# Planning the order of a whole kernel by repeated list scheduling, with new weights for its operations

## The chip, the cores and the metric

The kernel runs on one core of one Trainium2 chip. The metric is the time of one launch on the device, in microseconds (us). Five engines work side by side, each through its own instructions in the order in which they stand in the program: TensorE (PE, with its weight loads shown as PEld), VectorE (DVE), ScalarE (ACT), GpSimd (POOL) and SyncE (SP), which here only issues transfers. Engines wait for each other by semaphores.

## What is computed

Two layers over an input of shape (8, 192, 64, 64), that is 8 images of 192 channels and 64 by 64 places, all in float32. Cut to what matters:

```python
# layer 0: attention in windows of 8x8, only the 16 largest scores of each row, then an MLP
shortcut = layer_norm(tokens)
q, k, v  = windows(shortcut) @ qkv_w.T                 # 6 heads of 32
attn     = l2n(q) @ l2n(k).T * temperature
attn     = where(attn >= 16th largest of its row, attn, -100)
attn     = softmax(attn + relative_position_bias)
x2       = shortcut + (attn @ v) @ proj_w.T
x2       = x2 + gelu(layer_norm(x2) @ fc1_w.T) @ fc2_w.T
# layer 1: a small MLP on the 2-D Fourier coefficients of each channel, then an MLP
f  = fft2(layer_norm(x2))                              # over 64 x 64, each channel
x3 = x2 + real(ifft2(mlp_of(real(f), imag(f))))        # 2 -> 16 -> 2, gelu
out = x3 + gelu(layer_norm(x3) @ mlp1_w.T) @ mlp2_w.T
```

## The kernel before

An image is cut into 8 bands of 512 places (64 bands in all), and for the Fourier part into 12 groups of 16 channels (96 groups in all). The work is written as Python generators, the tasks:

- `front(b, i)`: turns the tokens of a band, normalises them, makes q, k and v, and the norms of q and k (three POOL calls of which the power of line 771 is the longest).
- `attention(b, i, hb)`, two per band: scales q and k, transposes them on DVE, scores on PE (tile `s`, line 879), the 16 largest by MAX8, MATCH_REPLACE8 and MAX8 on DVE (lines 907 to 911), mask, softmax over POOL, ACT, DVE and POOL (lines 919 to 929), transposes on PE (`at`, line 936) and the product with v (`po`, line 961).
- `back(b, i)`: projection (`pp`), the MLP of layer 0 (`mh_b`, `mo_b`), and the row statistics that layer 1 needs.
- `forward`, `pointwise` (twice) and `inverse` of a group: the Fourier transform by matrix products (`fa`, `fz`), the small MLP (`fh`, `fo`) and the way back (`fb`, `fy`). A `forward` of an image needs all 8 bands of the image.
- `leave(b, j)`: the MLP of layer 1 (`mh_d`, `mo_d`) and the output of a band. It needs all 12 groups of the image.

For images after the first, the MLP's input is turned over to channels by 32 by 32 transposes on DVE and a round trip through DRAM on the SP queue (`lt` to `lr` to `hn`, lines 571 to 585); on the first image's layer 0 it is turned on PE.

A task yields an operation before it emits the instructions of it. An operation names its engine, or two of them of which one is chosen (`EITHER` is ACT or DVE), its weight, and the units that it takes and gives back: four PSUM tiles `ps`, five `att`, seven `h`, two `hn`, two `xa`, one `qk` and so on. A weight is the planner's duration, in units of 10 ns. PE's operations carry a mode (`full`, `row64`, `row32`, `col32`, `s`, `v`), the part of the array that they use, and ACT's carry their table (`gelu` or `exp`).

`issue(streams, units)` keeps a model clock for each engine. At each step it looks at the next operation of every live task, works out when it could begin, and takes one: on each engine, among those that can begin within 15 units of the first, that with the least `begin + cost + urgency - 100 if it frees a PSUM tile`, and then the engine whose choice begins first. Urgency is 360 times the task's place in the sequence of images, so a band is worth 45 units. What is taken is emitted at once and never weighed again. The streams limit how many tasks of a kind are live: three attentions, two `back`, two `pointwise`, two `leave`, one of each other. The model adds 20 units where PE changes its mode and 130 where ACT changes its table, 30 from PE to another engine, 15 from others, and 210 after SP. Where two engines could do an operation, it goes to the one that ends first, with 40 units added for DVE.

Of the kernel before, what the change touches and what calls it, by code (L numbers as in the profile page):

```python
# [28 lines left out]
def op(engine, weight, mode=None, get="", put="", after=None, done=None, put_too=""):  # L29
    return engine, weight, mode, get.split(), (put + " " + put_too).split(), after, done  # L30


def issue(streams, units):

    change = {"pe": 20, "act": 130, "dve": 0, "pool": 0, "sp": 0}
    arrives = {"pe": 30, "sp": 210}
    clock = {e: 0 for e in change}  # L40
    mode = {e: None for e in change}
    units = {name: [0] * n for name, n in units.items()}
    events = {}
    live = []

    def advance(task, value):
        try:
            found = task["gen"].send(value)
            while not isinstance(found, tuple):

                new = dict(task, gen=found, queue=None)
                live.append(new)
                advance(new, None)
                found = task["gen"].send(None)
            task["op"] = found
        except StopIteration:
            live.remove(task)
            if task["queue"] is not None:
                start(task["queue"])

    def start(queue):
        if queue[0]:
            gen, place = queue[0].pop(0)
            task = {"gen": gen, "queue": queue, "urgency": 360 * place, "last": (None, 0)}
            queue[1] += 1
            task["order"] = (queue[1], len(live), place)
            live.append(task)
            advance(task, None)

    for tasks, width in streams:  # L70
        queue = [list(tasks), 0]
        for _ in range(width):
            start(queue)
    while live:
        best, ready = {}, {}
        for task in live:
            engines, weights, kind, get, put, after, done = task["op"]
            if isinstance(engines, str):
                engines, weights = (engines,), (weights,)
            free = 0  # L80
            deps = [task["last"]] if after is None else after
            deps = [d if d[0] is None or d[0] in change else events.get(d) for d in deps]
            if any(d is None for d in deps):
                continue
            short = False
            for name in set(get):
                n = get.count(name)
                if len(units[name]) < n:
                    short = True
                    break  # L90
                free = max(free, sorted(units[name])[n - 1])
            if short:
                continue
            found = []
            for engine, weight in zip(engines, weights):
                begin = max(clock[engine], free)
                for source, end in deps:
                    if source is not None and source != engine:
                        end += arrives.get(source, 15)
                    begin = max(begin, end)  # L100
                new = kind and mode[engine] and kind != mode[engine]
                cost = change[engine] if new else 0
                found.append((begin + cost + weight, engine, begin, cost, task, weight))

            _, engine, *rest = min(found, key=lambda f: f[0] + 40 * (f[1] == "dve"))
            ready.setdefault(engine, []).append((engine, *rest))
        for engine, found in ready.items():
            first = min(begin + cost for _, begin, cost, *_ in found) + 15
            best[engine] = min(
                [  # L110
                    (
                        begin + cost + task["urgency"] - 100 * ("ps" in task["op"][4]),
                        task["order"],
                        f,
                    )
                    for f in found
                    for _, begin, cost, task, _ in [f]
                    if begin <= first
                ],
                key=lambda v: v[:2],  # L120
            )
        choice = min(best.values(), key=lambda v: (v[2][1], v[:2]))[2]
        engine, begin, change_cost, task, weight = choice
        _, _, kind, get, put, after, done = task["op"]
        for name in get:
            units[name].remove(min(units[name]))
        end = begin + change_cost + weight
        clock[engine] = end
        if kind:
            mode[engine] = kind  # L130
        for name in put:
            units[name].append(end + (150 if engine == "sp" else 15))
        task["last"] = (engine, end)
        if done:
            events[done] = (engine, end)
        advance(task, (engine, end))


@with_exitstack
def kernel(  # L140
# [7 lines left out]

# [66 lines left out]
    make_identity(nc, ident)  # L225
# [274 lines left out]
    def statistics(src, nm):  # L500
# [3 lines left out]
        for j in range(2):  # L504
            yield op("dve", 54 + 42 * j)
            for t in range(2):
                nc.vector.bn_stats(st[:, t, j, :], src(t, j))
# [5 lines left out]
    def normalized(to, pair, src, mv, nm):  # L513

        yield op("pool", 130)
# [8 lines left out]
        for j in range(2):  # L524
            done = yield op(EITHER, (72, 96), after=[shifted])
# [32 lines left out]
    def mlp(src, nm, w1, fc1_bias, w2, by_dma, then=None):  # L558
# [7 lines left out]
        if by_dma:  # L566
            ready = yield op("dve", 115, get="att turn", put="xa", after=last)
# [7 lines left out]
            yield op("sp", 220, put="att")  # L575
# [5 lines left out]
            yield op("sp", 130, get="hn", put="turn")  # L581
# [7 lines left out]
        else:  # L589
# [3 lines left out]
            done = yield op(EITHER, (80, 96), put="ps")  # L593
# [4 lines left out]
        def gelu(fp, ph, last):  # L598
            yield op("act", 138, "gelu", put="ps", after=[last], done=("gelu", nm, fp))
# [59 lines left out]
        for half in range(2):  # L659
            if half == 0:  # L660
                yield op("pe", 384, "full", get="ps", after=last)
                acc = psum(f"mo_{nm}")
            else:
                last = yield op("pe", 384, "full", put="h h h")
# [16 lines left out]
    def front(b, i):  # L681
# [16 lines left out]
        done = yield op(EITHER, (80, 96), put="ps")  # L698
# [13 lines left out]
        for part in range(2):  # L712
            weights = (100, 100) if part else (62, 67)
# [29 lines left out]
        def squares(p, pq):  # L743
            copied = yield op(EITHER, (80, 96), put="ps")
            copy(copied, qk[:, :, p, :], pq[:, :, : 2 * C])
            squared = yield op(("act", "pool"), (81, 150), get="xa")
# [5 lines left out]
            yield op("dve", 95, put="xa", done=("sq", b, i, p))  # L752
# [23 lines left out]
        def values(whole):  # L776
            done = yield op(EITHER, (80, 96), put="ps", after=[whole], done=("vv", b, i))
            copy(done, vv.rearrange("p t a c -> p t (a c)"), pv[:, :, : 2 * C])
# [77 lines left out]
    def attention(b, i, hb):  # L856

        nm = f"{b}_{i}_{hb}"
        scaled = yield op(("pool", "dve"), (195, 140), after=[("front", b, i, hb), "rpb"])
# [13 lines left out]
        yield op("pe", 55, "s", get="ps ps att", put="qkt")  # L873
# [13 lines left out]
        for k in range(2):  # L887
            done = yield op(EITHER, (49, 56), put="ps")
# [9 lines left out]
        for k0 in range(0, 12, 2):  # L898
            yield op("dve", 100, get="sm" if k0 == 0 else "")
# [12 lines left out]
        yield op("dve", 106)  # L912
        mask = small(shape, "mask", U8)
        nc.vector.tensor_tensor(mask, s, top[:, :, :, 15:16].to_broadcast(shape), ALU.is_lt)
        yield op("dve", 108)
        nc.vector.copy_predicated(s, mask, row(neg.unsqueeze(1).to_broadcast([128, 3, 4])))  # L916

        yield op("pool", 150)
        nc.gpsimd.tensor_tensor(s, s, top[:, :, :, 0:1].to_broadcast(shape), ALU.subtract)  # L919
        yield op("pool", 190)  # L920
        nc.gpsimd.tensor_tensor(s, s, rpb.unsqueeze(2).to_broadcast(shape), ALU.add)
        yield op("act", 85, "exp")
        nc.scalar.activation(s, s, AF.Exp)
        yield op("dve", 117)
# [3 lines left out]
        yield op("pool", 150, put="sm")  # L928
# [12 lines left out]
        moved = yield op(EITHER, (80, 96), put="ps")  # L941
# [3 lines left out]
        if hb == 0:  # L945
            yield op("pe", 53, "v", get="ps ot", put="att", after=[moved, ("vv", b, i)], done=("ot", b, i))
            ots[b, i] = strip("ot", 1, f"ot_{nm}")
        else:
            yield op("pe", 53, "v", get="ps", put="att " + held[b, i][1], after=[moved, ("ot", b, i)])
# [18 lines left out]
        done = yield op(EITHER, (72, 72), put="ps", done=("att", b, i, hb))  # L968
# [10 lines left out]
    def back(b, i):  # L979
# [28 lines left out]
        yield op("dve", 98, put="ps", after=[last, ("xt", b, i)])  # L1008
# [5 lines left out]
        def biased():  # L1014
            yield op("pool", 183, done=("biased", b, i))
# [5 lines left out]
        if i > 0:  # L1021
# [3 lines left out]
            98,  # L1025
# [19 lines left out]
        yield op("pool", 200, done=("in", b, i))  # L1045
# [9 lines left out]
    def forward(b, n):  # L1055

        nm = f"{b}_{n}"
        yield op("pool", 250, get="xf", after=[("in", b, i) for i in range(NB)] + ["layer1"])
# [9 lines left out]
        yield op("pe", 90, "full", get="ps fa", put="xf")  # L1068
# [9 lines left out]
        yield op("dve", 70, put="ps")  # L1078
# [11 lines left out]
        yield op("pe", 100, "row32", get="ps ps fz", put="fa")  # L1090
# [13 lines left out]
        for k in range(2):  # L1104
            yield op("dve", 43 + 33 * k, put="ps", done=("fz", b, n) if k else None)
# [10 lines left out]
    def pointwise(b, n, half):  # L1116
# [4 lines left out]
        def gelu(hf, k, ph):  # L1121
            yield op("act", 111, "gelu", put="ps", done=("fh", nm, hf, k))
# [3 lines left out]
        for hf in range(2):  # L1126
            yield op(
                "pe",
                86,
# [21 lines left out]
        if half == 1:  # L1151
# [3 lines left out]
            172,  # L1155
# [19 lines left out]
        done = yield op(EITHER, (40, 43), put="ps", done=("fo", b, n, half))  # L1175
# [204 lines left out]
```

## Time and profile before

| what | value |
|---|---|
| median of 3 runs | 4767.55 us (4763.53 to 4770.57) |
| the profiled execution's own time | 4769.61 us |
| its span, first to last instruction | 4767.8 us |
| mean granted TensorE clock | 0.975 of full |
| PE busy | 4482.1 us, 94% |
| DVE, ACT, POOL busy | 2636.5, 2598.7, 2365.0 us: 55%, 55%, 50% |
| instructions | 143910 |

Busy time is the time in which an engine had an instruction under way. Matmuls overlap, so the mean length of one matmul is longer than the distance from one to the next. The profiled execution's own time is 1.8 us more than its span; sums below are made against it. The waits view lists for each group of instructions the time that its engine had been idle just before them, and what ended it; "issue" stands for idle time in which nothing that the profile shows was waited for. The granted clock is either full or half at a time; a value between is the mean over a stretch.

### The profile page before, as it was taken

Reading aid. Unit: us, or ns where it says so; the run is one execution under the profiler, and the core shown is the slowest. Engines: PE = TensorE matmul, PEld = TensorE weight load, DVE = VectorE, ACT = ScalarE, POOL = GpSimd, SP = SyncE. Lnnn points to the kernel's source line nnn. Section 1 sums busy time; section 2 is a strip of 40 time slices with the busy share of each in tenths; the row PEclk is TensorE's granted clock in tenths of the full one; section 3 lists DMA queues with packets and bytes.
Section 4 is the critical chain, followed back from the end, with each engine's and each line's share of the span. In section 5 each row is a group of like instructions: output and inputs, shape, how many; then the busy total and the mean of one; then the engine's idle time right before and its main releaser. Section 6 shows DMA issues by size and latency. Waiting matters only on the chain.

```text
span 4767.8 us, 143910 instructions
## 1 busy us (share of the span) xinstructions
PE 4482.1 (94%) x61178; PEld 3563.0 (75%) x61178; DVE 2636.5 (55%) x10804; ACT 2598.7 (55%) x3821; POOL 2365.0 (50%) x2189
## 2 busy tenths in 40 slices
PE   6787998999999999999999999999999999999989
PEld 4676776887778767787768876788777877778758
DVE  6776657464664655664564646655566465553111
ACT  4455656356654566545674456645566456643553
POOL 6677555355454555454573545546456355541200
PEclk7888999999999999999999999999999999999999
DMA  2000001110012100111011200121001210011002
GB/s 57 11 8 11 26 15 35 51 45 22 19 35 64 35 19 19 44 51 38 16 29 44 59 24 16 29 66 45 13 22 36 60 42 15 18 39 57 9 16 66
DMA packets 190428, 158.31 MB, mean 33 GB/s; under 512 B 31023, under 2 KB 157178, under 8 KB 189786
## 3 DMA queue, kind: packets, MB, share of 16 engines
q1 hardware_dynamic: 189774, 149.11, 11.2%
q8 instruction: 481, 7.88, 0.7%
q14 instruction: 161, 1.32, 0.1%
q10 hardware_dynamic: 12, 0.00, 0.0%
HBM read 76.48 MB, written 72.35 MB: 31 GB/s over the span
## 4 chain that ended last, share of the span: by engine, by line
PE 74%; DVE 9%; POOL 6%; ACT 5%; DMA 2%; issue 2%; SPq 1%; ACTq 0%; DVEq 0%; POOLq 0%
PE mo_b L668 10%; PE mo_d L668 9%; PE mh_b L622 7%; PE mh_d L622 7%; PE fh L1141 6%; PE fo L1168 6%; PE mh_b L635 4%; PE mh_d L635 3%; PE pq L787 3%; POOL nrm L771 3%; ACT fh L1124 2%; PE fa L1071 2%; PE fb L1189 2%; PE pp L989 2%; PE fy L1216 2%
## 5 line engine op out<-in xcount | busy, mean ns | idle before, releaser
L1124 ACT ACTIVATE fh<-fh,ab 128x1024 f32<-128x1024 f32 x768 | 813.0, 1111 | 298.4 <-PE fh L1141 294.8
L919 POOL TENSOR_TENSOR s<-s,top 128x768 f32<-128x768 f32 x128 | 191.5, 1496 | 762.2 <-DVE s L916 557.5
L771 POOL TENSOR_TENSOR nrm<-nrm,mhalf 128x24 f32<-128x24 f32 x128 | 555.6, 4340 | 10.7
L668 PE MATMUL mo_b<-wfc,h_b 128*128 128x192 f32 x3072 | 522.3, 329 | 1.5 <-DVE xn L852 1.0
L668 PE MATMUL mo_d<-wmlp,h_d 128*128 128x192 f32 x3072 | 515.0, 327 | 1.1 <-ACT fh L1124 1.1
L668 PEld LDWEIGHTS mo_b<-wfc,h_b 128*128 128x128 f32 x3072 | 501.5, 191 | 15.9 <-issue 10.4
L668 PEld LDWEIGHTS mo_d<-wmlp,h_d 128*128 128x128 f32 x3072 | 499.4, 190 | 12.6 <-issue 7.0
L1141 PE MATMUL fh<-fz,w1p 32*128 32x248 f32 (+1 forms) x6144 | 462.0, 405 | 16.3 <-ACT fh L1124 10.9
L1141 PEld LDWEIGHTS fh<-fz,w1p 32*128 32x128 f32 x6144 | 292.8, 186 | 147.3 <-issue 75.0
L622 PE MATMUL mh_b<-hn_b,wfc_a 128*128 128x256 f32 x1536 | 377.2, 393 | 24.3 <-DMA hn_b<-lr_b 19.8
L1168 PE MATMUL fo<-fh,w2p 128*32 128x264 f32 (+1 forms) x6144 | 388.4, 389 | 5.3 <-ACT fh L1124 4.8
L622 PE MATMUL mh_d<-hn_d,wmlp_a 128*128 128x256 f32 x1536 | 367.7, 387 | 21.2 <-DMA hn_d<-lr_d 18.7
L606 ACT ACTIVATE h_d<-mh_d,fcb 128x512 f32<-128x512 f32 x384 | 240.6, 686 | 255.0 <-PE mh_d L635 209.7
L622 PEld LDWEIGHTS mh_b<-hn_b,wfc_a 128*128 128x128 f32 x1536 | 286.1, 193 | 91.1 <-issue 31.3
L622 PEld LDWEIGHTS mh_d<-hn_d,wmlp_a 128*128 128x128 f32 x1536 | 283.3, 191 | 82.5 <-issue 39.8
L929 POOL TENSOR_TENSOR s<-s,rsum 128x768 f32<-128x768 f32 x128 | 196.0, 1534 | 257.8 <-DVE rsum L927 163.3
L909 DVE MATCH_REPLACE8 s<-top,s 128x64 f32<-128x64 f32 x1536 | 309.6, 209 | 0.0
L1168 PEld LDWEIGHTS fo<-fh,w2p 128*32 128x32 f32 x6144 | 185.5, 111 | 164.0 <-issue 41.0
L606 ACT ACTIVATE h_b<-mh_b,fcb 128x512 f32<-128x512 f32 x384 | 242.1, 689 | 116.1 <-PE mh_b L635 76.3
L907 DVE MAX8 top<-s 128x8 f32<-128x64 f32 x1536 | 256.7, 208 | 64.7 <-ACT s L852 64.0
L911 DVE MAX8 top<-s 128x8 f32<-128x64 f32 x1536 | 265.3, 214 | 0.0
L1254 DVE TENSOR_TENSOR zt<-mo_d,xy 128x768 f32<-128x768 f32 x64 | 61.2, 956 | 325.9 <-PE mo_d L668 325.9
(213 smaller groups left out, 8616.4 us busy)
## 6 DMA issues: line engine op xcount, KB each, us to landing
lr_d<-lt_d SPq DMA_DIRECT2D x256, 96.0 KB
lr_b<-lt_b SPq DMA_DIRECT2D x224, 96.0 KB
xin<-in_x SPq DMA_DIRECT2D x64, 256.0 KB
hn_d<-lr_d SPq DMA_DIRECT2D x64, 256.0 KB
out<-z SPq DMA_DIRECT2D x64, 256.0 KB
hn_b<-lr_b SPq DMA_DIRECT2D x56, 256.0 KB
xin<-in_x SPq DMA_DIRECT2D x128, 64.0 KB
hn_d<-lr_d SPq DMA_DIRECT2D x128, 64.0 KB
```

Source lines behind the costliest of these rows:

```text
L606: nc.scalar.activation(to, of, AF.Gelu, bias=fc1_bias[:, 2 * fp + k : 2 * fp + k + 1],)
L622: nc.tensor.matmul(ph[:, t, k * HALF : (k + 1) * HALF], w1[0][:, f], hn[:, t * HALF : (t + 1) * HALF], start=(first and k == 0), stop=not ...
L635: nc.tensor.matmul(ph[:, t, k * HALF : (k + 1) * HALF], w1[1][rows, f], hn[rows, BAND:ROW], start=(first and k == 0), stop=not first, skip ...
L668: nc.tensor.matmul(acc[:, j, t * C : (t + 1) * C], hs[f // 2][:, f % 2, q * 128 : (q + 1) * 128], w2[:, f, ORDER[t]], start=(f == 0 and t ...
L771: nc.gpsimd.tensor_tensor(nf, nf, mhalf[:, :24], ALU.pow)
L907: nc.vector.max(best[:, 0:8], of)
L909: nc.vector.match_replace(s2, best[:, 0:8], of, -3.0e38)
L911: nc.vector.max(best[:, 8:16], s2)
L929: nc.gpsimd.tensor_tensor(s, s, row(rsum), ALU.mult)
L1124: nc.scalar.activation(hs[hf, k], ph, AF.Gelu, bias=ab[:, 0:1])
L1141: nc.tensor.matmul(phs[k // 2][:, k % 2, cols], w1p[i][rows, hf].rearrange("p h v -> p (h v)"), fz[rows, :] if rhs is None else zu[rows, : ...
L1168: nc.tensor.matmul(po[rows, :] if i == 0 else pou[rows, :, 1 : U - 1], w2p[i][:, hf].rearrange("p a v -> p (a v)"), hs[hf, k // 2][:, k % ...
```

## The change

The order is no longer found while the program is emitted. The tasks are run twice. In the first run they run against a stand-in that swallows every call (`Mute`), and `listed` writes down each operation with its units and the operations that it waits for. `Plan` then schedules this list, and in the second run `issue` only replays the plan.

`Plan.run` is a list scheduling with the same key as before, with two differences: a random number can be added to the key of each operation, and within a stream a task may not overtake the task before it. `Plan.search` goes through the time of the plan in steps of 2000 units (20 us). For each it makes 40 schedules of the next 4000 units (40 us), the first without noise and 39 with normal noise of 25 units. It counts the PE weight scheduled inside the 40 us, and 0.15 of the weight on the other engines, and keeps the schedule with the largest sum; at the very end, the one that ends first. Of the chosen schedule it fixes the first 20 us and goes on from there. The weight counted leaves out the cost of a change of mode.

All weights and latencies are new. The work itself, its tiles, buffers, unit counts and stream widths stay as they were. The core of the diff:

```diff
-    change = {"pe": 20, "act": 130, "dve": 0, "pool": 0, "sp": 0}
-    arrives = {"pe": 30, "sp": 210}
+CHANGE = {"pe": 19, "act": 128, "dve": 0, "pool": 0, "sp": 0}
+ARRIVES = {"pe": 22, "dve": 18, "act": 15, "pool": 11, "sp": 265}
...
+                end = self.end[d] + (ARRIVES[source] if source != engine else 145 * (source == "sp"))
...
+    def run(self, until, noise=None):
...
+            for task, (number, begins) in ready.items():
+                a = front[task]
+                if a is not None and at[a] <= at[task]:
+                    continue
...
+                    key = begin + cost + place[task] - (100 if "ps" in put else 0)
+                    if noise:
+                        key += noise(number)
...
+    def search(self, tries=40, step=2000, horizon=4000, spread=25):
+        draw = random.Random(1)
+        now = 0
+        while self.ready:
+            now = max(now, self.clock["pe"])
+            kept, best = self.save(), None
+            for k in range(tries):
+                seed = draw.random()
+                noise = drawn(seed, spread) if k else None
+                if not self.run(now + horizon, noise):
+                    self.restore(kept)
+                    continue
+                worth = 0
+                for _, _, engine, begin, weight in self.log[kept[-1]:]:
+                    part = min(weight, max(0, now + horizon - begin))
+                    worth += part if engine == "pe" else 0.15 * part
+                if not self.ready:
+                    worth = 1e9 - max(self.clock.values())
+                if best is None or worth > best[0]:
+                    best = worth, seed if k else None
+                self.restore(kept)
+            seed = best[1]
+            self.run(now + step, drawn(seed, spread) if seed is not None else None)
+            now += step
...
+def issue(streams, plan):
+    tasks = Tasks(streams)
+    for name, engine, number in plan:
+        tasks.advance(name, (engine, number))
...
+    streams, units = program(Mute(), Mute(), x, out, w)
+    ops, of_task, made = listed(streams, units)
+    plan = Plan(ops, of_task, made, units, [width for _, width in streams]).search()
+    streams, _ = program(ctx, tc, x, out, w)
+    with tc.manual_schedule():
+        issue(streams, plan)
...
-            done = yield op(EITHER, (72, 96), after=[shifted])
+            done = yield op(EITHER, (89, 58), after=[shifted])
...
-            yield op("sp", 220, put="att")
+            yield op("sp", 200, put="att")
...
-            yield op("sp", 130, get="hn", put="turn")
+            yield op("sp", 100, get="hn", put="turn")
...
-            yield op("act", 138, "gelu", put="ps", after=[last], done=("gelu", nm, fp))
+            yield op("act", 115, "gelu", put="ps", after=[last], done=("gelu", nm, fp))
...
-                yield op("pe", 384, "full", get="ps", after=last)
+                yield op("pe", 390, "full", get="ps", after=last)
...
-        scaled = yield op(("pool", "dve"), (195, 140), after=[("front", b, i, hb), "rpb"])
+        scaled = yield op(("pool", "dve"), (148, 98), after=[("front", b, i, hb), "rpb"])
...
-            yield op("dve", 100, get="sm" if k0 == 0 else "")
+            yield op("dve", 90, get="sm" if k0 == 0 else "")
...
-            yield op("act", 111, "gelu", put="ps", done=("fh", nm, hf, k))
+            yield op("act", 100, "gelu", put="ps", done=("fh", nm, hf, k))
```

## The prediction, made before the changed kernel had run

> **What bounds the kernel now.** I read the page first, for the share of each engine.
>
> ```profile
> span 4767.8 us, 143910 instructions
> PE 4482.1 (94%) x61178; PEld 3563.0 (75%) x61178; DVE 2636.5 (55%) x10804; ACT 2598.7 (55%) x3821; POOL 2365.0 (50%) x2189
> PE   6787998999999999999999999999999999999989
> PEclk7888999999999999999999999999999999999999
> ```
>
> PE is the bound: 94% busy, no other engine above 55%. An order changes no product, so only what lies around the products can go. The table of stages says where PE stands still and where its clock is low:
>
> ```profile
> core 0: us, PE busy (x) PEld busy (x) DVE busy (x) ACT busy (x) POOL busy (x), PEclk, DMA share, GB/s
> 0.00:480.00 480.00, 371.44 (x4311) 293.40 (x4312) 335.81 (x1447) 233.93 (x391) 335.94 (x294) 0.84 0.09 22
> 480.00:4320.00 3840.00, 3696.43 (x51764) 2935.73 (x51748) 2216.43 (x9097) 2171.16 (x3163) 1972.83 (x1817) 0.99 0.12 34
> 4320.00:4768.00 448.00, 414.22 (x5130) 333.88 (x5128) 84.26 (x261) 193.62 (x268) 56.25 (x79) 0.98 0.12 35
> ```
>
> PE is idle for 480 - 371.4 = 108.6 us at the start, 3840 - 3696.4 = 143.6 in the middle, 448 - 414.2 = 33.8 at the end: 286 us. The clock's record has TensorE at half clock for 147, 78.5 and 17 us of these stages; work under way there takes twice as long, so at most 73, 39 and 9 us are lost.
>
> Next, PE's waits; first two lines from the start, then five from the middle, one from the end:
>
> ```profile
> PE at L936 <- POOL s L929: 52.7, 8, 12.1
> PE s L879 <- DVE qkt L869: 19.2, 10, 5.0
> ...
> PE mh_b L622 <- DMA hn_b<-lr_b: 17.2, 12, 2.5
> PE fb L1199 <- issue: 12.6, 13, 1.9
> PE at L936 <- ACT fh L1124: 12.0, 8, 2.9
> PE s L879 <- issue: 10.6, 7, 1.7
> PE fh L1141 <- ACT fh L1124: 10.2, 26, 1.0
> ...
> PE mh_d L622 <- DMA hn_d<-lr_d: 12.9, 1, 12.9
> ```
>
> The start waits for one chain, the softmax of few attentions. The middle has no large wait: many small ones, mean 0.4 to 1.5 us, the sort that an order decides. The two "issue" rows, 23.2 us, belong to no operation that a plan knows.
>
> The third loss is inside PE's busy time. PE's timeline:
>
> ```profile
> 2507.11 8.07 PE L668 MATMUL mo_b<-wfc,h_b 128*128 128x192 f32 x48
> 2515.11 1.15 PE L1141 MATMUL fh<-fz,w1p 32*128 32x264 f32 x16
> ```
>
> A whole second product (two operations, new weight 390 each, 7.80 us) took 8.00 us between two other modes: 0.20 us for one stay in a mode, near the planner's 19 or 20 units. Reading the whole timeline of PE by mode I count 2036 changes: 2036 x 0.19 = 387 us. Adding up the new weights, a band has 4482 units (front 740, attentions 376, back 192, MLPs 1554 and 1620) and a group 1134; with 528 units more on image 0 that is 64 x 4482 + 96 x 1134 + 528, or 3962 us. 3962 + 387 + 121 of clock + 286 idle is 4756, close to the span: the account closes, and some 400 us of changes and 286 of idle are what an order can reach.
>
> [...] half-clock stretches come in pieces of 3.4 us or multiples, after idle. [...] DVE's scaling of q and k (L864) takes 0.96 us as median, 1.41 as mean, 2.23 at worst. The planner knows nothing of this. [...] an exponential begins 1.29 us after the start of its load [...] and the planner's 128 units fit.
>
> **The change part by part.**
>
> *Nothing is added or removed* but a rare choice of engine: every product, copy and transfer stays. So PE's 3962 us stay.
>
> *Weights.* On DVE:
>
> ```profile
> 2408.27 0.34 DVE L907 MAX8 top<-s 128x8 f32<-128x64 f32 x2
> 2409.18 0.33 DVE L907 MAX8 top<-s 128x8 f32<-128x64 f32 x2
> ```
>
> From one pair of rows to the next is 0.91 us: the new 90 is right, the old 100 was a tenth too slow. Likewise a gelu of `fh` starts 1.01 us after the one before (two take 2.12, one 1.11): new 100, old 111. Old plans saw DVE and ACT some 10% busier than they are, and the chip ran ahead of them. The opposite held on SP:
>
> ```profile
> 2535.02 1.80 SPq L580 DMA_DIRECT2D lr_d<-lt_d  x4
> 2539.12 0.34 SPq L583 DMA_DIRECT2D hn_d<-lr_d  x1
> 2539.50 1.09 SPq L585 DMA_DIRECT2D hn_d<-lr_d  x2
> ```
>
> From the first write to the end of the last read's issue is 5.57 us, as the read waits for the write to land. The old plan took 220 + 130 = 3.5 us, the new one 200 + 145 + 100 = 4.45; with the arrival it has 7.10 us against 5.60. PE's waits for hn should shrink (23 us in the middle, 15.6 at the end).
>
> *Search.* In 40 us of the middle there are 1.5 us of idle (143.6 / 96) and 17 changes (3.2 us). The best of 40 random orders gains where orders differ: idle mostly. It counts only the first half of what it chose for good, then chooses again. I choose:
>
> - middle idle: 143.6 - 23.2 = 120.4 can be planned; 45% goes: -54. Ends: -20% (-24), -65% (-78).
> - middle half clock follows the idle: 38% of 39: -15 (-6 to -21).
> - start: the chain of three attentions and one `qk` is not widened, so a fifth of 108.6 and of 73: -22 and -15 (0 to -55 together).
> - changes: the sum counts PE weight without their cost, so orders with fewer win, but each is wanted by some data: 4% of 387: -15 (+8 to -31).
> - end: half of the hn waits: -8 (0 to -15).
> - thinner margin: PE has 33 operations per band and 10 per group, 3072. Where the old plan believed an engine slower, its result lay ready; now PE arrives as it is due. DVE's normalising call is 0.374 us as median and 0.449 as mean, so a step of two calls comes 0.15 us late on average. If it strikes 270 steps that is +40; from 0 to 1000 steps (a third of all), 0 to +150.
>
> Where DVE gains work (normalising by 58 against ACT's 89, scaling 98 + 40 against POOL's 148) nothing is added: DVE is idle 45% of the time; without that cover each step costs its 0.6 or 1 us.
>
> SP is passed too: the loads of x are issued inside `front` and cost nothing in either plan. They lie behind hn's reads when both meet, 1.7 us of issue; SP spends hundreds of us waiting, so I put this at 0, with +5 as bound. POOL's norms take 4.9 us a call and hold up what stands behind (a softmax, a row statistic); the new plan prices them as before, so 0, with 10 either way.
>
> Sum: -54 - 15 - 37 - 15 - 8 + 40 = -89. Against the profiled execution, 4769.6 - 89 = 4680.6. That execution is 2.1 us over the median, so **4680** stands for a median too. What is late next: PE's changes and the "issue" gaps, which stay.
>
> **The rivals.**
>
> - *Likeliest* (48%): as above, 4640 to 4720.
> - *The margin was what helped* (slower, 13%): the old, pessimistic weights left each result ready before PE's turn. For it: the middle has only 3.7% idle, and DVE's calls scatter up to 2.2 us. Against it: an order is not a clock; PE's queue doesn't wait for a planned time. With 1000 late steps the sum is -129 + 150 = +21, or 4790. It decides from 129 / 0.15 = 860 late steps on.
> - *The search finds gains that exist in the model only* (17%): what differs between 40 orders is smaller than the model's error, and only the repaired weights help: hn -19 (half of 38.6), -20 elsewhere: 4730.
> - *The search does more* (15%): the far ends of idle and clock (-99), of the start (-55), of changes (-31), -8 and a margin of +15: 4592.
> - *No change* (7%): [...] the plan trades one wait for another: 4768.
>
> **How the numbers follow.** The first, third and fourth give faster, 0.80. No change gives 0.06 within 0.2% (9.5 us, about what a measurement of this kernel can tell from no change), and the rest goes to slower with the second: 0.14. The range runs from the fourth's 4590 to a little over the second: 4795.
>
> **What would show it.** Right: PE's idle in the middle near 100 us, "DMA hn" rows below half, PE's busy time down by 30 to 60 us (clock and changes), start idle below 95, clock 0.98. The margin rival: more rows of PE waiting for DVE and ACT, each short, idle above 143. Model only: changes down, yet idle as before. Wrong altogether: a new long wait on one stream, as no task may now overtake its forerunner, or PE's busy time up.

## The result, and the profile after

The changed kernel takes 4739.31 us (median of 4 runs, 4739.15 to 4739.62) against 4768.05 us of the kernel before: a ratio of 0.9941, interval 0.9924 to 0.9958. It is 28.7 us faster where 89 were forecast: the right direction and inside the range, but a third of the size. The page of the changed kernel, the lines that answer to those shown of before:

```profile
span 4737.4 us, 143887 instructions
PE 4464.9 (94%) x61178; PEld 3535.0 (75%) x61178; DVE 2674.5 (56%) x10910; ACT 2517.1 (53%) x3690; POOL 2373.6 (50%) x2196
PE   6898999999999999999999999999999999999988
PEclk8999999999999999999999999999999999999999
```

The span is 30.4 us shorter; PE's busy time fell by 17.2 us and its idle time by 13.2 (285.7 to 272.5). The table of stages (columns: stretch, length, busy time of PE, PEld, DVE, ACT and POOL, granted clock, DMA share, GB/s) says where:

```profile
0.00:480.00 480.00, 393.44 (x4710) 314.11 (x4712) 369.58 (x1616) 249.05 (x425) 369.49 (x318) 0.91 0.11 26
480.00:4320.00 3840.00, 3692.28 (x51903) 2916.09 (x51903) 2225.95 (x9052) 2098.57 (x3029) 1962.69 (x1815) 1.00 0.12 34
4320.00:4768.00 448.00, 379.15 (x4569) 304.78 (x4567) 78.95 (x243) 169.50 (x237) 41.43 (x64) 0.97 0.13 37
```

At the start PE idles 86.6 us (before: 108.6). In the middle it idles 147.7, 4 us more than before. At the end, which here stops at 4737.4, it idles 417.4 - 379.2 = 38.2 (33.6 to its own end before). Time at half clock went from 147 to 89 us at the start, from 78.5 to 31 in the middle, and from 17 to 25 at the end. Counting only the part of it in which PE had work under way, it went from 92 to 46, from 65 to 31 and from 7 to 10. The waits of PE, two lines each of start and middle, one of the end:

```profile
PE at L1120 <- POOL s L1113: 28.5, 8, 8.0
PE s L1063 <- DVE qkt L1053: 23.8, 10, 6.1
...
PE mh_d L806 <- DMA hn_d<-lr_d: 16.7, 16, 2.1
PE fa L1255 <- POOL xf L1249: 13.2, 18, 2.2
...
PE mh_d L806 <- DMA hn_d<-lr_d: 22.6, 5, 13.7
```

The wait for the softmax chain at the start halved. The waits for `hn` did not shrink: those of layer 0 nearly left the list, those of layer 1 took their place, 42.1 us in all (with 2.8 of `hn_b`) where before had 38.6. And the middle has the same idle in other pieces. Adding up PE's timeline of the middle by length of wait (from 0.15 us on): waits of 2 us and more fell from 33.7 to 11.4 us, waits of 1 to 2 us from 46.4 to 42.9, waits under 1 us rose from 58.8 to 88.0 us. The clock rose from 0.99 to 1.00 although the idle did not fall; that the missing long waits are the reason fits this and was not tested by itself.

### The profile page after: what moved, and what is told of

The parts are those of the page before. It is cut to its first block, busy times and chain, and to the rows that moved or that the text cites. A ratio compares the mean times of both kernels' runs of the same rounds, so it can differ in the third digit from the quotient of the medians.

```text
span 4737.4 us, 143887 instructions
## 1 busy us (share of the span) xinstructions
PE 4464.9 (94%) x61178; PEld 3535.0 (75%) x61178; DVE 2674.5 (56%) x10910; ACT 2517.1 (53%) x3690; POOL 2373.6 (50%) x2196
## 4 chain that ended last, share of the span: by engine, by line
PE 53%; DVE 11%; POOL 8%; ACT 5%; issue 2%; DMA 2%; SPq 1%; ACTq 0%; DVEq 0%; POOLq 0%
PE mh_d L806 7%; PE mo_d L852 7%; PE fh L1325 5%; PE mo_b L852 5%; PE fo L1352 5%; PE mh_d L819 4%; PE mh_b L806 4%; POOL nrm L955 3%; ACT fh L1308 2%; PE mh_b L819 2%; PE pq L971 2%; DVE s L1093 2%; PE fa L1255 1%; DMA hn_d<-lr_d 1%; PE fz L1280 1%
## 5 line engine op out<-in xcount | busy, mean ns | idle before, releaser
L1325 PE MATMUL fh<-fz,w1p 32*128 32x264 f32 (+1 forms) x6144 | 460.2, 402 | 14.0 <-ACT fh L1308 7.6
L806 PE MATMUL mh_d<-hn_d,wmlp_a 128*128 128x256 f32 x1536 | 365.8, 388 | 42.1 <-DMA hn_d<-lr_d 39.4
L1352 PE MATMUL fo<-fh,w2p 128*32 128x264 f32 (+1 forms) x6144 | 378.7, 382 | 7.9 <-ACT fh L1308 3.7
L701 POOL TENSOR_SCALAR rs_d<-mv_d 128x4 f32<-128x4 f32 x64 | 14.6, 229 | 731.5 <-DVE mv_d L694 730.5
L806 PEld LDWEIGHTS mh_d<-hn_d,wmlp_a 128*128 128x128 f32 x1536 | 285.7, 192 | 105.9 <-issue 62.7
L1091 DVE MAX8 top<-s 128x8 f32<-128x64 f32 x1536 | 256.7, 208 | 59.6 <-ACT s L1036 58.8
```

What stands on the lines that cost most here:

```text
L806: nc.tensor.matmul(ph[:, t, k * HALF : (k + 1) * HALF], w1[0][:, f], hn[:, t * HALF : (t + 1) * HALF], start=(first and k == 0), stop=not ...
L1091: nc.vector.max(best[:, 0:8], of)
L1325: nc.tensor.matmul(phs[k // 2][:, k % 2, cols], w1p[i][rows, hf].rearrange("p h v -> p (h v)"), fz[rows, :] if rhs is None else zu[rows, : ...
L1352: nc.tensor.matmul(po[rows, :] if i == 0 else pou[rows, :, 1 : U - 1], w2p[i][:, hf].rearrange("p a v -> p (a v)"), hs[hf, k // 2][:, k % ...
```

## The experiments

Each kernel was timed beside the kernel before on the same chip; before had medians of 4765 to 4773 us there, so the ratio counts. "The plan's own clock" is the end of the planner's model, which comes from running the planner's code alone; it is a model and is used only to be set against measured spans. An "exact" weight is one of the change, taken from the median times of the trace; "old" weights are those of the kernel before, many of them too long.

**Search or weights?** The first run keeps the old `issue` and takes only the new numbers; the second keeps the new planner without its search; the third keeps the search and puts all old numbers back.

```diff
# weights alone: issue() of before, with
-    change = {"pe": 20, "act": 130, "dve": 0, "pool": 0, "sp": 0}
-    arrives = {"pe": 30, "sp": 210}
+    change, arrives = CHANGE, ARRIVES
# no search
-    def search(self, tries=40, step=2000, horizon=4000, spread=25):
+    def search(self, tries=1, step=2000, horizon=4000, spread=25):
# old weights: every op() as in before, and
-ARRIVES = {"pe": 22, "dve": 18, "act": 15, "pool": 11, "sp": 265}
+ARRIVES = {"pe": 30, "dve": 15, "act": 15, "pool": 15, "sp": 210}
```

> The old planner, one pass, with the new weights and latencies: the weights alone. If the repaired weights make the gain (the rival 'gains in the model only'), this comes to 4740, as the whole change does. If the search makes it, 4760 to 4768. If the thinner margin costs (exact weights leave nothing ready ahead of time), it is slower than before: 4780 or more, with more short waits of PE.

> The new planner with one schedule for each step in place of 40, so no search: weights, latencies and the rule that no task overtakes its forerunner stay. If the search makes the gain, 4755 to 4770; if the weights make it, 4740. Against the run with weights only it shows what the rule against overtaking costs: 0 if nothing, 10 or more if it binds. Idle of PE at the start should be back near 108 us if it was the search that shortened it.

> The search with the old, longer weights and old latencies. If the lost margin is what ate the gain, this beats the change: 4700 to 4725, with fewer short waits of PE in the middle. If right weights matter to the search, it falls back: 4750 to 4765. If the search works on its own and the weights hardly matter: 4735 to 4745.

Measured: 4758.06 us (ratio 0.9986, 0.9979 to 0.9992), 4771.75 (1.0014, 1.0007 to 1.0022) and 4689.73 (0.9847, 0.983 to 0.9863). New weights alone are worth 7 us: no gain like the change's, and no loss from a thinner margin either. The new planner without its search is 14 us slower than that, more than the 10 named as the sign that the rule against overtaking binds; with one order each, the rule is not shown to be the reason. The search makes the gain, and with the old, too long weights it makes 76 us, two and a half times that of the change. Without search the start is as it was, by the table of stages of the second run: PE idles 108.3 us there.

```profile
0.00:480.00 480.00, 371.74 (x4438) 292.50 (x4442) 336.27 (x1498) 245.48 (x414) 342.98 (x296) 0.86 0.09 23
```

**Luck of the draw?** The search draws random numbers, so I gave the change two other seeds and the old weights one.

```diff
-        draw = random.Random(1)
+        draw = random.Random(2)      # and 3
```

> The change with another seed of the random numbers, nothing else. If the 50 us between the change and the search with old weights are luck of the draw, this lands at 4690 to 4710. If they are margin, at 4720 to 4740.

> The change with a third seed. As for the second: luck 4690 to 4710, margin 4720 to 4740. The three together show how far one draw differs from another: the plan's own clock differs by 21 us over them.

> The search with old weights and old latencies with another seed. If the margin makes it faster, 4675 to 4700 again; if the first was luck, 4715 to 4740.

Measured: 4698.19 (0.9849, 0.9835 to 0.9864), 4714.44 (0.9884, 0.9869 to 0.9899), and 4670.43 with old weights (0.9787, 0.9773 to 0.9802). Draws of one search differ by 41 us, more than most edits, and the change as it stands is the worst of its three: their mean is 4717. My expectation that margin would hold the second seed at 4720 or more missed. Old weights stay ahead in both draws, by seed and in the mean (4680).

**Which margin?** Latencies longer, the rest exact; then DVE's and ACT's weights a tenth longer, the rest exact, with both seeds; then each engine by itself.

```diff
# latencies
-ARRIVES = {"pe": 22, "dve": 18, "act": 15, "pool": 11, "sp": 265}
+ARRIVES = {"pe": 42, "dve": 38, "act": 35, "pool": 31, "sp": 415}
# weights, in op(); also with "dve" alone and with "act" alone
+    engines = tuple((e, w * 11 // 10 if e in ("act", "dve") else w) for e, w in engines)
```

> The change with its exact weights, but every latency raised: 0.2 us more after PE, DVE, ACT and POOL, 1.5 us more after SP. If the missing margin ate the gain, this lands where the old weights with the search did: 4680 to 4700, with short waits of PE in the middle (under 1 us) at 45 us or less, against 75.6 in the change. If the old weights won by something else (their proportions, or luck of the draw), it stays at 4725 to 4745.

> The change with every weight of DVE and ACT a tenth longer, its latencies and all other weights exact. If too short a time on DVE and ACT is what the search exploits, this recovers what the old weights did: 4680 to 4700, PE idle in the middle near 105 us. If the old weights won by their latencies or their proportions, it stays at 4710 to 4740.

> The change with DVE's weights alone a tenth longer. DVE is the engine whose calls scatter most [...]. If DVE carries the effect, 4670 to 4690; if ACT does, 4710 to 4740.

> The change with ACT's weights alone a tenth longer. If ACT carries the effect (ACT empties most of what PE fills), 4670 to 4690; if DVE does, 4710 to 4740. Both in part: each 4690 to 4715.

> DVE and ACT a tenth longer, second seed: a second draw of what gave 4669.6 with the first seed. If the padding does it, 4650 to 4685, and below 4698, which the change gave with this seed; if the first draw was luck, 4695 to 4720.

Measured: latencies 4712.04 (0.9881, 0.9865 to 0.9898), though waits under 1 us in the middle did fall, from 88.0 to 50.5 us (the expectation counted fewer of them); DVE and ACT 4669.6 (0.9782, 0.9768 to 0.9797) and with the second seed 4671.73 (0.9794, 0.9779 to 0.9809); DVE alone 4669.17 (0.979, 0.9774 to 0.9807); ACT alone 4713.26 (0.9879, 0.9862 to 0.9896). A tenth on DVE's weights recovers it all: one draw with DVE alone and two with ACT as well lie within 3 us. Latencies and ACT, one draw each, end where the change's own draws do. The table of stages with DVE's tenth:

```profile
0.00:480.00 480.00, 400.96 (x4955) 312.42 (x4956) 347.14 (x1567) 263.01 (x444) 353.81 (x308) 0.90 0.10 24
480.00:4320.00 3840.00, 3732.47 (x52005) 2967.49 (x52003) 2193.28 (x8999) 2174.59 (x3211) 1990.14 (x1846) 1.00 0.12 35
```

PE idles 107.5 us in the middle, 40 less than in the change. Waits under 1 us are 54.6 us there. They are no mark of the lost margin by themselves: the change's second and third seeds have 66 and 56 us, before 58.8. What sets the kernels apart is who ended PE's waits in the middle. Added up from the waits view, DVE ended 30, 22 and 18 us of them in the change's three draws and 23 with ACT's tenth, but 9, 11 and 7 in the three kernels with DVE's tenth, and 10 and 7 with old weights (28 in the kernel before, which has old weights and no search; 30 with longer latencies). ACT ended 48 us with ACT's tenth, where the change has 50. So with a search on exact weights PE does stand and wait for DVE, and slack on DVE removes that.

Two rivals. Longer DVE weights also move work to ACT (10745 calls on DVE with DVE's tenth, 10910 in the change). But DVE and ACT both a tenth longer leave 10887 and 10891 there and gain as much, so the share of the work on DVE is not the reason. That the search's sum also counts DVE's longer weights, at 0.15, was not tried by itself.

**Is it DVE's wait for POOL?** DVE's calls do scatter. In the changed kernel's timeline of all engines, a pair of normalising calls ends 0.12 us after POOL's second call, 2.69 us after its own start, and a pair that meets none takes 0.64 us, a quarter of that:

```profile
2007.78 1.50 POOL L1103 TENSOR_TENSOR s<-s,top 128x768 f32<-128x768 f32 x1 [0.81 <-DVE s L1100]
2008.59 2.69 DVE L719 TENSOR_SCALAR xa_d<-xy,mv_d,rs_d 128x192 f32<-128x192 f32 x2
2009.36 1.81 POOL L1105 TENSOR_TENSOR s<-s,rpb 128x768 f32<-128x768 f32 x1
...
2054.98 0.64 DVE L719 TENSOR_SCALAR xa_d<-xy,mv_d,rs_d 128x192 f32<-128x192 f32 x2
```

The groups by line show that the change puts 406 such calls on DVE (before: 282) and that their mean is far over their median of 374 ns:

```profile
L719 DVE TENSOR_SCALAR xa_d<-xy,mv_d,rs_d 128x192 f32<-128x192 f32 x188 | 78.8, 474 | 69.4 <-POOL rs_d L702 63.8 <-PE pz L735 5.6
L719 DVE TENSOR_SCALAR xa_b<-xt,mv_b,rs_b 128x192 f32<-128x192 f32 x122 | 59.1, 536 | 29.8 <-POOL rs_b L702 29.6
L719 DVE TENSOR_SCALAR xt<-xt,mv_a,rs_a 128x192 f32<-128x192 f32 x96 | 45.5, 525 | 36.6 <-POOL rs_a L702 36.6
```

In the same trace each of the 46 normalising calls of over 0.9 us on DVE ends 105 to 119 ns after a POOL call of over 1 us: this is the contention. So I put back the two old weights of the calls that it makes longer, and then, as that also moves ACT's and POOL's weights, set DVE's alone to the means of the trace, with two seeds.

```diff
# old normalise
-            done = yield op(EITHER, (89, 58), after=[shifted])
+            done = yield op(EITHER, (72, 96), after=[shifted])
-        scaled = yield op(("pool", "dve"), (148, 98), after=[("front", b, i, hb), "rpb"])
+        scaled = yield op(("pool", "dve"), (195, 140), after=[("front", b, i, hb), "rpb"])
# means
-            done = yield op(EITHER, (89, 58), after=[shifted])
+            done = yield op(EITHER, (89, 90), after=[shifted])
-        scaled = yield op(("pool", "dve"), (148, 98), after=[("front", b, i, hb), "rpb"])
+        scaled = yield op(("pool", "dve"), (148, 121), after=[("front", b, i, hb), "rpb"])
-            yield op("dve", 34 + 22 * k, put="ps", done=("fz", b, n) if k else None)
+            yield op("dve", 34 + 51 * k, put="ps", done=("fz", b, n) if k else None)
```

> The change with two old weights alone: normalising 72 on ACT and 96 on DVE (the change: 89 and 58), scaling q and k 195 on POOL and 140 on DVE (148 and 98). [...] the change puts 406 normalising calls on DVE where before had 282. If that contention is the cause, 4690 to 4705 with about 290 calls on DVE; if it is margin in general, 4715 to 4740.

> The change with three DVE weights set from the median to the mean of what its trace shows: normalising 58 to 90, scaling 98 to 121, the second half of fz 56 to 85. All others exact. If DVE's padding works because these three calls are priced too short [...], 4670 to 4690. If the slack is what helps, wherever it lies, 4700 to 4735.

> The same three weights with the second seed, where the change gave 4698 and DVE and ACT a tenth longer gave 4672. Pricing of three calls: 4660 to 4685. Slack in general: 4690 to 4720.

Measured: 4726.73 (0.9903, 0.9886 to 0.992), 4710.59 (0.9878, 0.9864 to 0.9893) and 4707.69 (0.9867, 0.985 to 0.9883). All lie among the change's own draws, the first with only 272 normalising calls on DVE. DVE still ended 15, 21 and 16 us of PE's waits in the middle. Right means for the calls that scatter do not help beyond these draws; a tenth on every DVE weight does.

**More search.** First a shorter step with exact weights; then a stronger search with old, with exact, and with padded weights (seeds 3, 3 and 8; seed and search for old and for padded weights were picked among some tens of plans as the one whose own clock ended first).

```diff
-    def search(self, tries=40, step=2000, horizon=4000, spread=25):
+    def search(self, tries=40, step=1000, horizon=4000, spread=25):     # first
+    def search(self, tries=100, step=1000, horizon=3000, spread=20):    # the other three
```

> The search fixes 10 us at a time and not 20, so it chooses twice as often; the plan's own clock then ends 35 us earlier than that of the change. If the chip follows the plan, 4705. If only a third of what the plan promises arrives, 4727. If the search mostly fits orders to errors of the model, 4735 to 4745.

> Old weights and latencies, a stronger search (100 schedules of 30 us for each 10 us, noise 20, third seed), chosen since its plan's own clock ends at 4625 us. Plans with old weights ended on the chip 10 to 14 us of span later than they said, so 4637 to 4645 of launch time. If that agreement was chance, 4660 to 4690.

> The same stronger search and seed with the exact weights and latencies of the change. Its plan's own clock ends at 4610 us, earlier than that of the plan with old weights. If the margin matters, it is slower all the same: 4690 to 4710, against 4640. If the search alone matters, about the same or 10 us faster.

> DVE and ACT a tenth longer and the stronger search (100 schedules of 30 us for each 10 us, noise 20), eighth seed, chosen since its plan's own clock ends earliest of those tried, at 4611 us. Padded plans ended on the chip 10 to 29 us of span later than they said: 4625 to 4645 of launch time, the fastest of all. If the exact weights' failure with this search comes from the search, 4680 or more.

Measured: 4685.18 (0.9834, 0.9816 to 0.9852), 4660.13 (0.9766, 0.9751 to 0.978), 4743.42 (0.9939, 0.9925 to 0.9954) and **4637.05 (0.9713, 0.9694 to 0.9733)**, which beats both kernels. The first beat all three expectations; as one draw of a search whose draws spread by 41 us it decides nothing. (DVE ended 30 us of PE's waits there all the same; its start is 40 us less idle than before.) The second and third have the same search and the same seed:

| kernel | plan's own clock | span | span less plan |
|---|---|---|---|
| the new planner without search | 4694 us | 4766.8 us | 72 |
| the change | 4629 | 4737.4 | 108 |
| its seeds 2 and 3 | 4615, 4608 | 4694.1, 4705.3 | 79, 97 |
| exact weights, shorter step | 4595 | 4676.1 | 81 |
| exact weights, stronger search | 4610 | 4739.8 | 130 |
| latencies longer | 4683 | 4704.1 | 21 |
| DVE a tenth longer | 4628 | 4668.7 | 41 |
| DVE and ACT a tenth longer, seeds 1 and 2 | 4649, 4648 | 4671.0, 4669.6 | 22, 22 |
| old weights, seeds 1 and 2 | 4670, 4650 | 4683.5, 4660.2 | 14, 10 |
| old weights, stronger search | 4625 | 4653.4 | 29 |
| DVE and ACT a tenth longer, stronger search | 4611 | 4635.5 | 25 |

The spans are those of the profiled executions; the medians of the launches lie up to 10 us above them. Longer weights and latencies make the plan itself later, so a small distance is in part made by them: longer latencies bring it to 21 us too, but their plan is 54 us longer than the change's, and their kernel has 61 more changes of mode than before. The fair pair is the change and DVE's tenth: their plans end within 2 us of each other, their spans 69 us apart. With exact weights some 72 us are missing even without a search; the search adds to that. With exact weights the stronger search's plan ends 19 us before that of the change and 2 us after that of its third seed, and on the chip it is no faster than either; with padded weights it brings 33 us. That is one draw each. The stages' middle lines and PE's largest wait there, first exact, then padded:

```profile
480.00:4320.00 3840.00, 3673.89 (x51119) 2919.19 (x51118) 2228.75 (x8976) 2104.51 (x3055) 1949.86 (x1800) 0.99 0.12 34
PE mh_d L806 <- DMA hn_d<-lr_d: 33.1, 19, 5.6
```

```profile
480.00:4320.00 3840.00, 3754.61 (x52354) 2997.57 (x52354) 2261.82 (x9131) 2149.23 (x3104) 1994.53 (x1848) 1.00 0.12 35
PE mh_d L807 <- DMA hn_d<-lr_d: 12.4, 12, 2.6
```

166 us of idle against 85. The transfer of `hn` starts from DVE's transposes (in the changed kernel's trace SP's queue waits for them 72 times, 1364 us in all); that its lateness comes from there is likely, not shown.

## Why the prediction was wrong, point by point

The forecast was -129 us of gains and +40 for the lost margin. The runs give each its size. Padded on DVE, or on DVE and ACT, with this very search, the gain is 99, 104 and 97 us against before on the same chip: 100. The three draws with exact weights gain 29, 72 and 56: 52.

The terms can also be read from the traces one by one, for the change and for DVE's tenth. A change of mode is put at 0.19 us: in the traces of both kernels, where PE did not wait, the first matmul after a change starts 0.19 us as median (mean 0.20, mostly 0.09 to 0.30) later than the next of the same product would have. The clock's term is half the time at half clock with work under way: two matmuls of the second product (`mo_b`) start 320 ns apart there and 163 ns at full clock (medians, the same in both traces).

| term, us | forecast | the change | DVE a tenth longer |
|---|---|---|---|
| start, idle | -22 | -22.0 | -29.6 |
| start, clock | -15 | -23 | -14 |
| middle, idle | -54, and +40 of margin | +4.1 | -36.1 |
| middle, clock | -15 | -17 | -20 |
| changes of mode | -15 | +3 | +6 |
| end, idle and clock | -8 | +6 | -1 |
| sum | -89 | -49 | -94 |
| span, measured | | -30.4 | -99.1 |

- *Gains, -129 forecast, -100 measured.* **The terms for changes of mode and for the end failed**, -15 and -8, **and the largest term, the middle's idle, was too big.** PE's timeline has 2051 changes, 15 more than before (+3 us), and over the searched runs between 2002 and 2097 (before: 2036): the search does not save them. At the end the change has 4.6 us more idle; its waits for `hn` grew from 15.6 to 22.6 us. The middle's idle, -54 forecast without the lost margin, falls by 36 to 40 in the three kernels with DVE's tenth. The start and the middle's clock gave somewhat more than forecast.
- *Thinner margin, +40 forecast, 48 measured* (100 - 52, two means of three draws, where those with exact weights differ by 43). The prediction was right that exact weights cost margin, but only together with a search: without one they cost nothing (7 us faster). Its working was not right: 270 steps at 0.15 us from the normalising calls should have gone away when those calls were priced at their mean, and did not. The slack of all of DVE is what counts.
- *Draw, not in the forecast, 23* (29 gained against 52 in the mean). It needed a term, with at least 20 us to both sides. That the change drew the worst of its three orders is bad luck; the 52 of the mean would still fall 37 short.
- From -89 to -29: gains 29 short, margin 8 more, draw 23. These are differences of the same measurements and must add up; the check is the table. It closes to 5 us with DVE's tenth. In the change 19 us are missing from the gain.
- *Start, -22 and -15*: idle right at -22.0; half clock -23, half as much again as forecast.
- *Middle clock, -15*: right at -17, although the idle from which it was worked out did not fall; that half clock goes down with the sum of the idle was an estimate.
- *Waits for hn below half*: wrong, 38.6 to 42.1 us. With the new weights alone they did fall, to 25.3; in the searched orders of the change they are back (42, 43 and 41 in its three draws), and 43 with the old price of the transfer too. Why is not shown.
- *The account of the time before* closed at 4756 us only because the clock's loss was put at its bound of 121 us. With work under way it is 82, and some 50 us of the span are not accounted for.
- *The rival "the margin was what helped"* named the mechanism, and its sign came true (the middle's idle above 143); it put it too strong: 48 us do not outweigh 100. *"Gains in the model only"* is out as it was put, since weights alone give 7 us and the search more. A part of it holds: against the run without search, the mean plan of the three draws is 77 us shorter and the mean span 54.

Two things stay open. Why slack on DVE works and the same slack on ACT does not is not shown. Of the two, DVE is the one whose calls scatter: in the changed kernel's trace 130 of its 10910 last over 1.5 times the median of their kind, of ACT's 3690 none does. The answers by line show it (shortest, median and longest in ns), a normalising call of DVE and a gelu of ACT:

```profile
L719 DVE TENSOR_SCALAR xa_d<-xy,mv_d,rs_d x188: 306/374/1972, 845.5 to 4693.9; 128x192 f32<-128x192 f32 x188
L1308 ACT ACTIVATE fh<-fh,ab x768: 1092/1114/1166, 433.0 to 4561.1; 128x1024 f32<-128x1024 f32 x192
```

This agrees with it, but taking the scatter itself away was not tried. And PE's busy time fell by 17 us although half clock under its work fell from 164 to 86 us, worth 39, with 3 us of changes added. These are the missing 19 us of the table; what they are, the profile does not say.

## What to carry to other kernels

A planner that only ordered took the median times of a trace without loss here. A search among orders did not get on the chip all that it got in its plan: 54 of 77 us with exact times. Try a tenth more on the engine whose times scatter; here that was worth more than any right price for single calls. Judge a search by several seeds before any edit to it, as seeds alone moved this kernel by 41 us. And set a plan's own end against the measured span before searching harder: here that paid where the two lay within some 25 us, and not where they were 80 to 110 us apart, one or two runs of each.

## What the runs showed of the hardware

A pair of normalising calls on DVE that meets two POOL calls takes 2.69 us instead of 0.64; in the changed kernel's trace all 152 pairs that met none of POOL's calls of over 1.2 us took 0.61 to 0.67 us. Normalising calls of over 0.9 us all end 105 to 119 ns after a POOL call of over 1 us: 46 of 46 there, 20 of 20 before. Unexpected was that pricing it right made no difference beyond that of the draws (4710.59 and 4707.69 us, where these lie from 4698 to 4739).

The clock's record holds full and half clock alone. Before, 32 of its 33 half-clock stretches begin after 1.0 to 3.4 us of PE idle within the 3.4 us ahead of them, in the change 18 of 20 after 1.6 to 3.4. The reverse holds less often: of the waits of 2 us and more in the middle, 9 of 13 before and 2 of 5 in the change saw half clock begin in them or within 3.4 us of their end. And where long waits of PE gave way to as much time in short ones, the granted clock of the middle went from 0.99 to 1.00: half-clock time there fell from 78.5 to 31 us with idle time up by 4. The sum of the idle alone does not tell it: with 107.6 us of idle in the middle, DVE and ACT both a tenth longer had a clock of 0.99, the change with 147.7 had 1.00.
